# A fused pass over 32 blocks: two of six answers added by VectorE ahead of TensorE, releases made by ScalarE, two scales computed at once

## The chip, the cores and the metric

The kernel runs on one core of a Trainium2 chip. The metric is the device time of one execution in microseconds; the number for a kernel is the median over several executions. The profile and the trace come from one more execution, taken by the hardware profiler.

## The reference

Two layers, each a graph network followed by a mixture of experts, over 128 graphs of 64 nodes with 256 channels: 8192 tokens. Cut to what matters here:

```
# layer 0
x1  = x + gnn0(norm(x), adj)                 # 256 -> 1024 -> 256, rms norm, silu
xn1 = norm(x1)
top, idx = top_k(xn1 @ gate.T, 6);  s = softmax(top)       # 64 experts, 6 of them per token
mix = sum_k  s[k] * (xn1 @ lattice[idx[k]])                # six answers per token
h   = xn1 + mix @ out_w.T + out_b
x2  = x1 + norm(h) * ln_g + ln_b
# layer 1
hn  = norm(norm(x2)) * gamma + beta
x3  = x2 + norm(x2) + relu((adj @ hn) @ W_rel + b_rel + hn @ W_root)
xn3 = norm(x3)
top, idx = top_k(xn3 @ Wg + bg + bias, 2);  w = softmax(top)   # 8 experts, 2 per token
out = x3 + sum_k w[k] * (relu(xn3 @ W1[idx[k]] + b1) @ W2[idx[k]] + b2)
```

## The kernel before, in words

The tokens are handled in 32 blocks of 256 (two tiles of 128 rows). There are four passes.

1. A first pass over the blocks computes the graph network of layer 0, chooses six experts for each token, and sends a copy of the token, with its destination and its release (the softmax weight), to a table in DRAM that is sorted by expert. Sends are indirect DMAs whose descriptors GpSimd writes (`send`, L334).
2. An expert pass walks over the pages of that table, multiplies each page by the matrix of its expert, scales by the release and replies: an indirect DMA puts each answer into its place in `answer` (L341), six rows per token, already weighted.
3. The fused pass, to which the change belongs, walks over the blocks again. For each block it reads the six answers of each token (`load_y`, L974), adds and transposes them on TensorE (`mixture`, L994: six matmuls against the identity that accumulate in one PSUM region), multiplies by `out_w` (`out_proj`), finishes layer 0 (`layer_out_h`, `_a`, `_b`, `_c`), does the graph network of layer 1 (`flip_h`, `neighbours`, `convolve_a`, `convolve_b`), and chooses two experts and sends two copies per token (`residual1_a`, `residual1_b`, `flip3`, `gate1`, `choose1`, `count1`, `place1`, `send1`). The release of a copy here is the difference of the two top logits (`differ`, L296); the sigmoid is taken in the last pass. Each block has four sends, one per tile and rank, and each send has its own `differ`.
4. A last pass walks over the pages of the second table: two matmuls per page with relu between them, and an indirect DMA that adds the result to the output (L351).

The order in the fused pass is written out by hand for TensorE, VectorE and ScalarE: `staggered` (L486) runs over steps, and in each step over a list of stages, each a function with a lag in blocks. In step s a stage with lag l works on block s - l, so the stages of one step belong to different blocks and the list gives the order of each of the three engines' instructions. One step makes one stage of each kind. The list is at L1143: `load_y` has lag -3, `mixture` -2, `out_proj` -1, `layer_out_a` to `_c` 0, `neighbours` and `convolve` 1, `residual1` and `gate1` 2, `choose1` and `place1` 3, the later three `send1` 4. The queues of SyncE (all loads and stores of the pass) and GpSimd (the sends) are ordered by the framework's planner, which goes by program order and by when it reckons things ready.

Buffers: a tile pool gives each name a number of rotating buffers; a stage that writes a tile waits until the readers of the buffer's former content are done. `y` (six answers of a block, 12 KB per partition) has two buffers. The loads of `y` for block 5 and later wait until all replies of the expert pass have landed (`READY`, L512); those before read rows that are known to be complete.

In `layer_out_b` ScalarE takes two square roots of the variance of x2 (`spread` at L1031, L1035), one for the plain norm and one for the norm of the norm. In `layer_out_c` VectorE makes a scale and a shift from each (`scale_shift`, L62: a reciprocal at L67 and a product at L68) and adds one to the first scale (L1042). ScalarE then writes `hn` and `s` (L1045, L1049).

Of the kernel before, what the change touches and what calls it, by code (L numbers as in the profile page):

```python
# [9 lines left out]
F32 = mybir.dt.float32  # L10
# [5 lines left out]
AF = mybir.ActivationFunctionType  # L16
ALU = mybir.AluOpType
AX = mybir.AxisListType
PSUM = bass.MemoryType.PSUM
P = 128  # L20
# [58 lines left out]
class Router:  # L79
# [213 lines left out]

    def differ(self, t, k, top, xs):

        self.nc.vector.tensor_sub(xs[:, t, k, self.D + 1:self.D + 2], top[:, t, 1 - k:2 - k], top[:, t, k:k + 1])  # L296

    def normalize(self, w, den):
        nc = self.nc
# [186 lines left out]
def staggered(n, stages, first=0):  # L486

    for s in range(first + min(lag for lag, _ in stages), n + max(lag for lag, _ in stages)):
        for lag, f in stages:
            if first <= s - lag < n:  # L490
                f(s - lag)
# [3 lines left out]
def two_layer_gnn_moe_kernel(ctx: ExitStack, tc: tile.TileContext, a: dict, out: bass.AP):  # L495
    nc = tc.nc
    x_in, adjT = a["x"], a["adjT"]
    N, D = x_in.shape
# [4 lines left out]
    T = 2  # L503
# [5 lines left out]
    K0 = 6  # L509
    E1, F1, _ = a["L1_ffn_W2"].shape  # L510
    EARLY = 12
    READY = 5  # L512
    LOOK = 20
    KF = F1 // P
    ctx.enter_context(tc.manual_schedule(engines={ENG.PE, ENG.DVE, ENG.Activation}))
# [2 lines left out]
    small = ctx.enter_context(tc.tile_pool(name="small", bufs=3))  # L518
# [9 lines left out]
    ops = Ops(nc, small, ident, eps)  # L528
# [42 lines left out]
    def load_adjacency(b):  # L571
        at = adjacency[b % 4]
        for g in range(2):
            nc.sync.dma_start(out=at[g * G:(g + 1) * G, :, g * G:(g + 1) * G],
                              in_=adjT[2 * b * T + g:2 * (b + 1) * T:2].rearrange("t m n -> m t n"))
        return at
# [27 lines left out]
    with tc.tile_pool(name="c0", bufs=1) as c0, \  # L604
# [9 lines left out]
        blocks = [dict() for _ in range(NB)]  # L614
# [151 lines left out]
        def place(b):  # L766
# [3 lines left out]
            send(b, 0)  # L770
            if b == READY - 1:
                r0.look_back()
            if b == LOOK:
                r0.look(EARLY)

        def send(b, k):

            B = blocks[b]
            r0.release(k, *B["w"], B["xs"])
            r0.send(B["row"], B["xs"], b > LOOK, (k,))  # L780

# [46 lines left out]
        n = free[0] // 16  # L828
# [118 lines left out]
    with tc.tile_pool(name="c3", bufs=1, reuse_waits="tile") as c3, \  # L947
# [17 lines left out]
        blocks = [dict() for _ in range(NB)]  # L965
# [3 lines left out]

        def load_y(b):  # L970
            B = blocks[b]
            B["y"] = y = work.tile([P, T, K0, D], F32, name="y")
            for t in range(T):
                d = nc.sync.dma_start(out=y[:, t],  # L974
                                      in_=r0.answer[ts(b * T + t, P * K0), :].rearrange("(p k) d -> p k d", k=K0))
                if b < READY:
                    tc.declare_no_dep(d.ins, group="r0last", reason="in the first pages, or waited for above")

        def load3(b):
# [4 lines left out]
            nc.sync.dma_start(out=x1, in_=by_tile(x1_dram[b]))  # L984
            B["at"] = load_adjacency(b)

        def mixture(b):

            B = blocks[b]
            pt = psum.tile([P, KD, C], F32, name="ps")  # L990
            for t in range(T):
                for k in range(KD):
                    for i in range(K0):
                        nc.tensor.matmul(pt[:, k, ts(t, P)], lhsT=B["y"][:, t, i, ts(k, P)], rhs=ident,  # L994
                                         start=(i == 0), stop=(i == K0 - 1), is_transpose=True)
            B["accT"] = accT = work.tile([P, KD, C], F32, name="accT")
            nc.scalar.copy(accT, pt)

# [20 lines left out]
        def layer_out_b(b):  # L1019
            B = blocks[b]  # L1020
            h = B["h"]
            mv, rs = B["mvh"], B["rsh"]
            nc.vector.reciprocal(rs, rs)
            B["x2"] = x2 = work.tile([P, T, D], F32, name="x2")
            for t in range(T):
                nc.vector.scalar_tensor_tensor(h[:, t, :], h[:, t, :], mv[:, t, 0:1], ln_g,
                                               op0=ALU.subtract, op1=ALU.mult)
                nc.vector.scalar_tensor_tensor(x2[:, t, :], h[:, t, :], rs[:, t:t + 1], B["x1"][:, t, :],
                                               op0=ALU.mult, op1=ALU.add)
            B["mv2"] = mv = ops.stats(x2)  # L1030
            B["std2"] = ops.spread(mv)  # L1031


            B["rs2"] = rs2 = small.tile([P, T], F32, name="rs2")
            ops.std(rs2, mv[:, :, 1], 1e-10, 1.0 + 1e-5)  # L1035

        def layer_out_c(b):
            B = blocks[b]
            x2 = B["x2"]
            rs2, nm2 = ops.scale_shift(B["mv2"], B["rs2"])  # L1040
            rs, nm = ops.scale_shift(B["mv2"], B["std2"])
            nc.vector.tensor_add(rs, rs, one[:, :T])  # L1042
            B["hn"] = hn = work.tile([P, T, D], F32, name="hn")
            for t in range(T):
                nc.scalar.activation(hn[:, t, :], x2[:, t, :], AF.Identity, bias=nm2[:, t:t + 1], scale=rs2[:, t:t + 1])  # L1045

            B["s"] = s = work.tile([P, T, D], F32, name="s", bufs=3)
            for t in range(T):
                nc.scalar.activation(s[:, t, :], x2[:, t, :], AF.Identity, bias=nm[:, t:t + 1], scale=rs[:, t:t + 1])  # L1049
# [86 lines left out]
        def send1(b, i):  # L1136
# [4 lines left out]
            r1.send(B["row"], B["xs"], b > NB // 2, (k,), (t,))  # L1141

        staggered(NB, (  # L1143
            (-3, load_y),
            (-2, load3),
            (0, layer_out_h),
            (3, choose1),
            (-2, mixture),
            (1, flip_h),
            (3, count1),  # L1150
# [5 lines left out]
            (2, residual1_b),  # L1156
            (1, neighbours),
            (0, layer_out_b),
            (4, lambda b: send1(b, 3)),
            (1, convolve_a),  # L1160
            (2, flip3),
            (1, convolve_b),
            (2, gate1),
            (3, place1),
            (0, layer_out_c),
            (4, load_w2),
        ))
        r1.page_table(work.tile([P, 512], F32, name="scratch", bufs=1))
# [110 lines left out]
```

## Time and profile before

| | |
|---|---|
| median of 10 runs | 2055.2 us (2051.68 to 2060.04) |
| profiled execution | 2057.27 us, of which 2055.5 us are the span from the first to the last instruction |
| granted TensorE clock, mean | 0.972 |
| TensorE (PE) busy | 1926.8 us, 94% |
| TensorE weight loads (PEld) busy | 1678.8 us, 82% |
| VectorE (DVE) busy | 1199.6 us, 58% |
| ScalarE (ACT) busy | 1019.0 us, 50% |
| GpSimd (POOL) busy | 1164.2 us, 57% |
| fused pass, by the rows of L974 and L994 | from about 1132 us to about 1528 us of the span |
| busy in 1197.5 to 1474.0 us (276.5 us) | PE 276.36, DVE 250.92, ACT 178.79, POOL 106.04 us |

How to read it: the shares of the page are means over four passes with different limits, so they say little on one of them. The last row is the steady part of the fused pass alone. Busy time is the union of the instructions' spans; consecutive small instructions of one engine may overlap by some 0.08 us, and an instruction that needs the result of the one before it starts after that one's end. A busy PE is not TensorE at its peak, since its matmuls are pipelined. In rows of the timeline the columns are start and length in us, engine, line, operation, output and inputs with their shapes, the count, and in brackets the idle time of the engine just before and who ended it. In rows of the groups, the numbers after the bar are busy time in us and mean length in ns.

### The profile page before, as it was taken

What the parts mean: (1) busy time and instruction counts of PE and PEld (TensorE: products, weight loads), DVE (VectorE), ACT (ScalarE), POOL (GpSimd) and SP (SyncE); (2) the same over time, 40 slices, a digit from 0 to 9 for tenths busy, and PEclk for the clock granted to TensorE, in tenths of its full rate; (3) what the DMA queues carried; (4) which work ended last, traced back from release to release, by engine and by line L of the source; (5) the groups of instructions that cost most, each with busy time, mean ns of one, the idle gap of its engine ahead of it and who ended that gap; (6) DMA issues with size and microseconds to landing.
All of it is one profiled execution on the core that took longest, in us unless ns stands there. A gap on an engine that the chain in (4) does not pass through costs nothing. (4 is left out here: it accounts for less than half of the span.)

```text
span 2055.5 us, 37214 instructions
## 1 busy us (share of the span) xinstructions
PE 1926.8 (94%) x10516; PEld 1678.8 (82%) x10516; DVE 1199.6 (58%) x4205; ACT 1019.0 (50%) x2033; POOL 1164.2 (57%) x1134
## 2 busy tenths in 40 slices
PE   6999999999966989999999799999979999999996
PEld 5888888888864777888877688988868888888885
DVE  5899999999975333344333389999862222222221
ACT  4888888888841222222222266666643333333332
POOL 1377667767677777777777724333343444444443
PEclk9999999999977999999999899999989999999998
DMA  4244554544486988666665799788527666666664
GB/s 123 80 142 149 169 165 166 171 159 140 134 267 209 306 256 264 208 207 209 209 207 165 264 374 337 260 283 280 176 91 170 171 163 161 153 167 162 166 167 91
DMA packets 282561, 397.91 MB, mean 194 GB/s; under 512 B 56025, under 2 KB 236393, under 8 KB 282353
## 3 DMA queue, kind: packets, MB, share of 16 engines
q1 hardware_dynamic: 202880, 246.61, 39.4%
q0 software_dynamic: 64416, 136.14, 22.1%
q10 hardware_dynamic: 15056, 12.69, 1.9%
q8 instruction: 94, 1.54, 0.3%
q14 instruction: 115, 0.93, 0.2%
HBM read 222.84 MB, written 176.64 MB: 194 GB/s over the span
## 5 line engine op out<-in xcount | busy, mean ns | idle before, releaser
L334 POOL DMA_INDIRECT r0x<-xs,r0row x384 | 402.6, 1048 | 236.0 <-DVE lat L706 72.3
L341 POOL DMA_INDIRECT r0y<-px x404 | 393.4, 974 | 123.1 <-DMA r0y<-px 51.8
L918 PE MATMUL py<-lat,pxT 128*128 x1616 | 389.4, 384 | 16.6 <-ACT pxT L905 13.0
L351 POOL DMA_INDIRECT out_x<-py_s,px x138 | 215.1, 1559 | 294.5 <-DMA out_x<-py_s,px 203.0
L922 DVE TENSOR_SCALAR px<-py,px 128x256 f32<-128x256 f32 x404 | 176.9, 479 | 310.1 <-PE py L918 306.1
L918 PEld LDWEIGHTS py<-lat,pxT 128*128 128x128 f32 x1616 | 293.6, 192 | 57.4 <-ACT pxT L905 17.5
L905 ACT COPY pxT<-pt 128x512 f32<-128x512 f32 x202 | 118.1, 586 | 368.9 <-PE pt L903 252.0
L1217 ACT ACTIVATE phid<-ph,pw 128x256 f32<-128x256 f32 x276 | 130.9, 474 | 323.7 <-PE ph L1215 167.5
L1215 PE MATMUL ph<-pxT,pw 128*128 128x256 f32 x1104 | 251.5, 381 | 0.7 <-ACT pxT L1206 0.7
L1235 PE MATMUL py<-fw,phid 128*128 (+1 forms) x1104 | 249.8, 379 | 0.4 <-issue 0.4
L717 PE MATMUL ps<-lat 128*128 128x256 f32 x1024 | 238.5, 381 | 0.0
L1215 PEld LDWEIGHTS ph<-pxT,pw 128*128 128x128 f32 x1104 | 211.0, 191 | 30.1 <-ACT pxT L1206 1.1
L684 PE MATMUL ph<-lat 128*128 128x256 f32 x1024 | 232.4, 386 | 2.7 <-DVE lat L706 2.0
L1235 PEld LDWEIGHTS py<-fw,phid 128*128 128x128 f32 x1104 | 204.4, 190 | 25.6 <-issue 0.6
L334 POOL DMA_INDIRECT r1x<-xs,r1row x128 | 128.5, 1004 | 169.1 <-DVE xs L296 47.4
L684 PEld LDWEIGHTS ph<-lat 128*128 128x128 f32 x1024 | 195.2, 193 | 29.5 <-issue 2.4
L717 PEld LDWEIGHTS ps<-lat 128*128 128x128 f32 x1024 | 193.8, 192 | 24.9
L1229 DVE TENSOR_SCALAR p<-p 128x2 f32<-128x2 f32 x69 | 11.9, 172 | 224.4 <-ACT p L1228 224.4
L1238 DVE TENSOR_TENSOR py_s<-py,pb 128x512 f32<-128x512 f32 x69 | 47.8, 692 | 158.3 <-PE py L1235 149.7
L903 PE MATMUL pt<-ident,px 128*128 128x128 f32 x808 | 127.5, 277 | 12.4 <-DMA px<-r0x 12.0
L903 PEld LDWEIGHTS pt<-ident,px 128*128 128x128 f32 x808 | 101.1, 143 | 39.6 <-DMA px<-r0x 12.0
L994 PE MATMUL ps<-ident,y 128*128 128x128 f32 x768 | 96.3, 284 | 14.0 <-DMA y<-r0y 14.0
(303 smaller groups left out, 2981.9 us busy)
## 6 DMA issues: line engine op xcount, KB each, us to landing
px<-r0x SPq DMA_DIRECT2D x404, 129.0 KB
y<-r0y SPq DMA_DIRECT2D x64, 768.0 KB
pw<-in_L_ffn_W1b SPq DMA_DIRECT2D x69, 514.0 KB
px<-r1x SPq DMA_DIRECT2D x69, 258.0 KB
x<-x SPq DMA_DIRECT2D x64, 256.0 KB
pb<-in_L_ffn_b SPq DMA_DIRECT2D x69, 128.0 KB
r0x<-r0filler ACTq DMA_DIRECT2D x64, 129.0 KB
lat<-in_x SPq DMA_DIRECT2D x32, 256.0 KB
```

What stands on the lines that cost most here:

```text
L334: i = self.nc.gpsimd.indirect_dma_start(out=self.table[:, :], out_offset=bass.IndirectOffsetOnAxis(ap=row[:, t, k:k + 1], axis=0), in_=xs[ ...
L341: d = self.nc.gpsimd.indirect_dma_start(out=self.answer[:, :], out_offset=bass.IndirectOffsetOnAxis(ap=x[:, self.D:self.D + 1].bitcast(I32 ...
L351: i, d = f"{self.name}add{i}", self.nc.gpsimd.indirect_dma_start(out=self.total[:, :], out_offset=bass.IndirectOffsetOnAxis(ap=x[:, self.D ...
L684: nc.tensor.matmul(ph[:, c, :], lhsT=w1[:, k, ts(2 * j + c, P)], rhs=B["aggT"][:, k, :], start=(k == 0), stop=(k == KD - 1))
L717: nc.tensor.matmul(B["po"][:, t, :], lhsT=B["hT"][:, c, ts(t, P)], rhs=w2[:, c, :], start=False, stop=(t == T - 1 and c == KH - 1))
L903: nc.tensor.transpose(pt[:, k, ts(q, P)], Q["px"][:, q, ts(k, P)], ident)
L905: nc.scalar.copy(xT[:, :, :n * P], pt[:, :, :n * P])
L918: nc.tensor.matmul(py[:, q, :], lhsT=xT[:, k, ts(q, P)], rhs=lat[:, ds(regs["e"][(2 * j + q) % 4], 1), k, :].rearrange("p o d -> p (o d)") ...
L922: nc.vector.tensor_scalar(px[:, q, :D], py[:, q, :], px[:, q, D + 1:D + 2], None, op0=ALU.mult)
L1215: nc.tensor.matmul(ph, lhsT=w[:, k * F1 + c * P:k * F1 + (c + 1) * P], rhs=Q["xT"][:, k, :], start=(k == 0), stop=(k == KD - 1))
L1217: nc.scalar.activation(hid[:, c, :], ph, AF.Relu, bias=w[:, KD * F1 + c:KD * F1 + c + 1], scale=1.0)
L1235: nc.tensor.matmul(py[:, t, :], lhsT=Q["hid"][:, c, ts(t, P)], rhs=fw2[:, ds(e, 1), c, :].rearrange("p o d -> p (o d)"), start=(c == 0), s ...
```

## The change

- `load_y` moves from lag -3 to lag -4 and `y` gets a third buffer.
- A new stage `fold`, lag -3, last but one in the list (after `layer_out_c`). For blocks from 8 on, VectorE adds answers 4 and 5 of each token to answers 0 and 1, in place, in one instruction. `mixture` then accumulates four answers for these blocks instead of six.
- `differ` moves from VectorE (one subtraction) to ScalarE (one activation, -1 times the one logit plus the other as a bias).
- The two square roots of `layer_out_b` go into the halves of one tile; `layer_out_c` takes one reciprocal and one product over both halves instead of two each.

```diff
@@ differ
-        self.nc.vector.tensor_sub(xs[:, t, k, self.D + 1:self.D + 2], top[:, t, 1 - k:2 - k], top[:, t, k:k + 1])
+        self.nc.scalar.activation(xs[:, t, k, self.D + 1:self.D + 2], top[:, t, k:k + 1], AF.Identity,
+                                  bias=top[:, t, 1 - k:2 - k], scale=-1.0)
@@ constants
     READY = 5
+    FOLD = 2
@@ load_y
-            B["y"] = y = work.tile([P, T, K0, D], F32, name="y")
+            B["y"] = y = work.tile([P, T, K0, D], F32, name="y", bufs=3)
@@ before mixture
+        def fold(b):
+            B = blocks[b]
+            B["n"] = K0
+            if b > READY + 2:
+                B["n"] = n = K0 - FOLD
+                y = B["y"]
+                nc.vector.tensor_add(y[:, :, :FOLD], y[:, :, :FOLD], y[:, :, n:])
@@ mixture
-                    for i in range(K0):
+                    for i in range(B["n"]):
                         nc.tensor.matmul(pt[:, k, ts(t, P)], lhsT=B["y"][:, t, i, ts(k, P)], rhs=ident,
-                                         start=(i == 0), stop=(i == K0 - 1), is_transpose=True)
+                                         start=(i == 0), stop=(i == B["n"] - 1), is_transpose=True)
@@ layer_out_b
-            B["std2"] = ops.spread(mv)
-            B["rs2"] = rs2 = small.tile([P, T], F32, name="rs2")
-            ops.std(rs2, mv[:, :, 1], 1e-10, 1.0 + 1e-5)
+            B["std2"] = std = small.tile([P, 2, T], F32, name="std2")
+            ops.std(std[:, 0, :], mv[:, :, 1], 1e-5)
+            ops.std(std[:, 1, :], mv[:, :, 1], 1e-10, 1.0 + 1e-5)
@@ layer_out_c
-            rs2, nm2 = ops.scale_shift(B["mv2"], B["rs2"])
-            rs, nm = ops.scale_shift(B["mv2"], B["std2"])
+            both = small.tile([P, 2, T], F32, name="rs2")
+            nms = small.tile([P, 2, T], F32, name="nm2")
+            nc.vector.reciprocal(both, B["std2"])
+            nc.vector.scalar_tensor_tensor(nms, B["mv2"][:, :, 0].unsqueeze(1).to_broadcast([P, 2, T]), -1.0, both,
+                                           op0=ALU.mult, op1=ALU.mult)
+            rs, rs2 = both[:, 0, :], both[:, 1, :]
+            nm, nm2 = nms[:, 0, :], nms[:, 1, :]
             nc.vector.tensor_add(rs, rs, one[:, :T])
@@ the stages of the pass
-            (-3, load_y),
+            (-4, load_y),
...
             (0, layer_out_c),
+            (-3, fold),
             (4, load_w2),
```

## The prediction

> **What bounds the kernel now.** I first looked for the stretch that the change touches. The rows of L994, the reading of the answers, run from 1137.7 to 1476.1 us: the fused pass. The chain of waits there is TensorE alone, in steps of one period. One step of it:
>
> ```profile
> 1274.72 2.67 PE ps L994 x24
> 1277.39 0.44 PE ps L76 x4
> ...
> 1278.14 1.73 PE po L1005 x8
> 1279.87 1.73 PE pz L1066 x8
> ...
> 1284.84 0.92 PE pg L1112 x8
> 1285.77 0.27 PE ps L994 x2
> ```
>
> From one L994 to the next is 11.05 us with nothing of another engine between, so TensorE sets the step, and 24 matmuls in 2.67 us are 0.111 us each. That would make any cut of TensorE's work a gain. So next comes how near the other engines are, by stretches (columns: PE, PEld, DVE, ACT, POOL busy with counts, granted clock, DMA share, GB/s): a full step, and one at the end of the pass, when no answers are left to read.
>
> ```profile
> 1319.00:1330.00 11.00, 11.00 (x76) 9.85 (x75) 10.01 (x47) 7.10 (x16) 4.12 (x6) 1.00 0.81 262
> ...
> 1484.90:1495.70 10.80, 9.03 (x51) 7.31 (x50) 9.97 (x47) 6.28 (x15) 3.93 (x6) 1.00 0.21 73
> ```
>
> VectorE is busy 10.0 us of 11.0 in the full step, and what looks like 1 us of room is not room: many of its instructions start only when the one before has ended, some 0.03 us later. The timeline of VectorE shows the true room.
>
> ```profile
> 1328.10 0.39 DVE L327 CAST r1row<-r1rowf 128x4 int32<-128x4 f32 x1
> ...
> 1329.11 0.69 DVE L1011 TENSOR_TENSOR h<-po,xn 128x512 f32<-128x512 f32 x1
> 1329.99 0.17 DVE L1118 TENSOR_TENSOR logits<-pg,r_L_ffn_bg 128x16 f32<-128x16 f32 x1 [0.19 <-PE pg L1112]
> ...
> 1484.92 0.17 DVE L1118 TENSOR_TENSOR logits<-pg,r_L_ffn_bg 128x16 f32<-128x16 f32 x1 [0.22 <-PE pg L1112]
> ...
> 1494.58 0.16 DVE L67 RECIPROCAL bn_rs<-bn_sd 128x2 f32<-128x2 f32 x1
> 1494.77 0.16 DVE L68 SCALAR_TENSOR_TENSOR bn_nm<-bn_mv,bn_rs 128x2 f32<-128x2 f32 x1
> 1494.97 0.16 DVE L1042 TENSOR_TENSOR bn_rs<-bn_rs,one 128x2 f32<-128x2 f32 x1
> 1495.05 0.69 DVE L1011 TENSOR_TENSOR h<-po,xn 128x512 f32<-128x512 f32 x1
> 1495.66 0.16 DVE L1118 TENSOR_TENSOR logits<-pg,r_L_ffn_bg 128x16 f32<-128x16 f32 x1
> ```
>
> In a full step VectorE waits for another engine once, at the logits. From 1484.92 to 1495.66 it does the same 46 instructions while TensorE has no answers to read, and here the logits wait for nothing: 10.74 us is what VectorE needs for a step when nobody holds it. Its room in a full step is 11.05 - 10.74 = 0.31 us.
>
> **The change part by part.** *TensorE.* For blocks 8 to 31 the mixture reads four answers instead of six: 8 matmuls less, 8 x 0.111 = 0.89 us. TensorE's need falls to 11.05 - 0.89 = 10.16 us in 24 steps. That is all that is to be had, 21 us, and only if nothing else needs more than 10.16.
>
> *The fold, on VectorE.* One addition of 1024 elements per partition, both inputs in SBUF, float32. The same form is in the first pass (L694), and L1017 is its shorter relative:
>
> ```profile
> L694 DVE TENSOR_TENSOR lat<-lat 128x1024 f32<-128x1024 f32 x32 | 39.1, 1223 | 8.0 <-ACT lat L687 7.2
> ...
> L1017 DVE TENSOR_TENSOR x<-x,r_L_ffn_ln_b 128x512 f32<-128x512 f32 x25 | 16.5, 658 | 0.0
> ```
>
> It lasts 1.22 us. The next independent instruction starts 0.08 us before such a one ends (L1017 starts at 1323.24, lasts 0.66, its follower starts at 1323.82). So the fold takes 1.14 us of the queue; bounds 1.10 and 1.22. It is put behind the last scale of a step, so h, the logits, the choice and everything of the next step queue behind it, and TensorE's next mixture now waits for it. Its own wait, for an answer load issued a step earlier, is covered: in the steady steps nothing waited for y.
>
> *What leaves VectorE.* Four subtractions at L296: by the starts of the next instructions (0.04, 0.07, 0.05, 0.07 after them) 0.23 us, although each lasts some 0.15. And the scales: two reciprocals and two products become one each. From the first reciprocal (1494.19) to h (1495.05) is now 0.86 us; the new three instructions are the last three before h, 1494.58 to 1495.05, 0.47. Gain 0.39. Of this 0.12 is a stall: the cast at 1328.10 lasts 0.39 when a send's descriptors are written beside it (GpSimd from 1327.54 to 1328.51), 0.17 at 1195.15 when none are, and there the five instructions take 0.74. In the new order that send waits for ScalarE's release, made behind both square roots: by the row at 1493.46 that ends near 1493.95, and GpSimd starts sends about 0.28 later (1327.54 after 1327.26), 1494.2. The cast starts at about 1494.0 and ends before. I take the stall as gone; if it comes back, 0.12 more.
>
> VectorE's new need: 10.74 - 0.23 - 0.39 + 1.14 = 11.26 us (11.22 to 11.46). That is more than the 11.05 of now: in the 24 steps with a fold the step becomes VectorE's, and TensorE's 0.89 turns into a wait of 1.1 us per step at the mixture. 24 x 0.21 = +5.0 us (24 x 0.17 = +4.1 to 24 x 0.41 = +9.8).
>
> A rule against it is weighed here. L1017 lasts 658 ns in every step though a send's descriptors are being written during it (1322.52 to 1323.56), and L694 stayed at 1.22 with sends all around it, so I charge the fold nothing for GpSimd. The Trainium skill (SBUF — State Buffer, Who interferes with whom) says that a VectorE instruction with two SBUF inputs is blocked by a GpSimd instruction that reads SBUF. Were each fold held for one whole send of 0.97 us, the sum would be +28 us instead of +5.
>
> *ScalarE* gets four small activations: the 2-element ones last 0.29 and follow each other by 0.21, so 7.1 us become 7.9 to 8.3 of 11. One is on a path: the release of the fourth send stands between the square roots (1493.46) and the copy xn3T (1493.64), so gate and logits come 0.21 later. In the fold steps the logits have the fold ahead of them (1.14), which hides it. At the end it shows: steps 29 and 30 have no fold, VectorE needs 10.12, but gate ended at 1495.3 for logits possible at 1495.5, now 0.21 later and 0.11 earlier for the two subtractions ahead of it: about 10.7. Against 11.05 and 10.74 that is -0.4 in all (0 to -1.5).
>
> *SyncE.* A third buffer, loads of y one step earlier. In the filling of the pass TensorE waits for answers at 1159.35, 1163.59 and 1165.86 (0.40 + 0.78 + 0.73 = 1.9 us), which can shrink. But the load of block 5 is held until the last replies have landed (1181.28), and with the new order xn of block 3 (now issued at 1162.45) stands behind it; h of block 3 ran at 1184.50, with 1.06 us of idle after it. From -1.9 to +1.0; I take 0, since the load that gates it does not move. The DMAs are the same in number and bytes.
>
> **Sum.** +5.0 - 0.4 + 0 = +4.6. The profiled execution took 2057.27 us (span 2055.5 and 1.8 around it), 2.1 above the median of ten, 2055.2; the steps lost are the same in both, so the forecast is 2055.2 + 4.6 = 2059.8. Bounds: 4.1 - 1.5 - 1.9 = +0.7 and 9.8 + 1.0 = +10.8, so 2056 to 2066. About 0.2% (4.1 us) is what a measurement of this kernel can tell from no change, so this case alone lies on both sides of that line.
>
> **The rivals.** *Faster: the fold costs VectorE less than I charge.* VectorE's step is 10.12 plus the fold; at 0.93 us of fold nothing changes, and below that the kernel gains, down to TensorE's 10.16. At half my price (two elements a cycle, 0.61 us) the step is 10.73, 24 x -0.32 = -7.6: 2047; with a free fold 2034. For it: the operands lie in one tile, in long runs. Against it: L694 and L1017 both show one element per cycle. *The lock.* The cast, moved nearer to its send, is caught at the start of it: up to 0.97 us per step less the 0.17 of its own, 24 x 0.8 = +19, 2079. For it: 0.39 against 0.17 shows that it can be caught; against it: the 0.2 us between by the rows. *The clock.* TensorE, idle 1.1 us in 11.3, gets half its clock for a while. In the step after 1495.7 (TensorE idle 0.73 just before) the granted share is 0.84, and L1066 takes 3.06 us and L1077 2.36, 1.89 each in the steady steps. In the step before it a gap of 1.02 brought none:
>
> ```profile
> 1486.39 0.19 PE L217 MATMUL pos<-r1hot,r0tri 128*128 128x16 bf16 x2 [1.02 <-DVE r1hot L209]
> ```
>
> There TensorE was idle for over 1.7 us of 10.8, more than the fold steps leave; a slow stretch adds some 1.7 us to TensorE, of which 1.1 is covered, so 0.6 a step: +14, 2074. The Trainium skill (TensorE: Matmul & The Clock Gate, HAM oscillation) asks for gaps over about 3.4 us before the clock falls; the drop at the end of the pass came with gaps under 1.1 us.
>
> **How the numbers follow.** VectorE-bound as summed 0.77 (0.51 of it above +0.2%, 0.25 within, 0.01 below); faster by a cheaper fold 0.11; the lock 0.06; the clock 0.06. So slower 0.63, same 0.25, faster 0.12. The range takes the first case's bounds and reaches a little past them on both sides, 2054 to 2068, leaving out most of the three others.
>
> **What would show it.** Right: the period of L994 in the steady steps 11.2 to 11.4, TensorE with a wait of about 1 us for VectorE ahead of L994 in 24 steps, no wait of VectorE at the logits there, the fold at 1.22, the cast back at 0.17, granted clock 1.00. Wrong: a period under 11.0 (the fold or the removed work was mispriced), a cast of over 0.5, or a granted share below 1 in the steady steps.

## The result and the profile after

The median after is 2064.55 us (8 runs, 2062.09 to 2069.44) against 2055.62 us of the kernel before (28 runs with those taken beside it): +8.9 us, a ratio of 1.0047 with a 95% interval of 1.0038 to 1.0056. The change makes the kernel slower. The profiled execution took 2067.96 us, its span is 2066.1 us, and the mean granted clock is 0.974.

Line numbers after the diff are larger: the fold is L996, the mixture L1005, `out_proj` L1016, h L1022, the new scales L1053 and L1054, `xn3T` L1122, the gate L1128, the logits L1134, the cast L328, the release L296 (now on ScalarE).

The chain of waits in the fused pass, before a chain of TensorE alone, now reads so (start, length, what; one step):

```profile
1286.79 0.06 DVE y L996
1286.85 1.08 issue
1287.93 0.68 DVE h L1022
1288.62 0.09 DVE logits L1134
...
1295.06 0.48 DVE x L1039
```

Every piece of it is VectorE's. The 1.14 us of the first two lines are the fold: the "issue" is the rest of it, up to where h starts. Over the whole execution VectorE's share of the chain rises from 1% to 10% and TensorE's falls from 37% to 27%. The timeline of VectorE at the end of one step:

```profile
1297.43 0.17 DVE L328 CAST r1row<-r1rowf 128x4 int32<-128x4 f32 x1
1297.50 0.17 DVE L1053 RECIPROCAL rs<-std 128x4 f32<-128x4 f32 x1
1297.71 0.16 DVE L1054 SCALAR_TENSOR_TENSOR nm<-bn_mv,rs 128x4 f32<-128x4 f32 x1
...
1297.98 1.23 DVE L996 TENSOR_TENSOR y<-y 128x1024 f32<-128x1024 f32 x1
1299.13 0.68 DVE L1022 TENSOR_TENSOR h<-po,xn 128x512 f32<-128x512 f32 x1
1299.73 0.16 DVE L1134 TENSOR_TENSOR logits<-pg,r_L_ffn_bg 128x16 f32<-128x16 f32 x1
```

The fold lasts 1.23 us and occupies the queue for 1.15 (1297.98 to 1299.13). The logits, which ended the only wait of VectorE before, wait for nothing. The next logits come at 1310.93, 11.20 us later. TensorE has the gaps instead, two in each step:

```profile
1286.64 1.06 PE L1128 MATMUL pg<-m_L_ffn_Wg,xn3T 128*128 128x8 f32 x8 [0.34 <-ACT xn3T L1122]
1288.12 1.94 PE L1005 MATMUL ps<-ident,y 128*128 128x128 f32 x16 [0.42 <-PE pg L1128]
```

The second gap is put down to TensorE itself; the instruction that ended then is VectorE's fold (1286.79 plus 1.23 is 1288.02), whose end the mixture needs. By stretches (columns as above), a full step:

```profile
1309.90:1321.10 11.20, 10.45 (x68) 9.11 (x67) 10.48 (x42) 7.80 (x20) 4.49 (x5) 1.00 0.84 283
```

TensorE, busy 11.05 of 11.05 before, is busy 10.45 of 11.20, at full clock.

Where the time went, by the starts of the logits: in the 24 steps with a fold (third logits to 27th) 265.41 us before and 270.60 after, **+5.2**. From the first mixture to the third logits 70.75 and 71.87, **+1.1**. From the 27th logits to the last 51.16 and 52.02, **+0.9**. The fused pass begins 0.3 later, and the last pass begins 7.5 later in all. The rest, to 8.9, can't be placed: the last pass, whose code nobody touched, took 527.1 us in the profile before, 530.2 after, and between 526.2 and 534.7 in profiles of the experiments (all counted from its first product, `ph`).

### The profile page after: what moved, and what is told of

Same layout as the page of the kernel before. It is cut to its first block, busy times and chain, and to the rows that moved or that the text cites. A ratio compares the mean times of both kernels' runs of the same rounds, so it can differ in the third digit from the quotient of the medians.

```text
span 2066.1 us, 36720 instructions
## 1 busy us (share of the span) xinstructions
PE 1910.1 (92%) x10324; PEld 1658.6 (80%) x10324; DVE 1207.2 (58%) x4037; ACT 1039.9 (50%) x2161; POOL 1170.4 (57%) x1134
## 5 line engine op out<-in xcount | busy, mean ns | idle before, releaser
L335 POOL DMA_INDIRECT r1x<-xs,r1row x128 | 134.9, 1054 | 177.8 <-ACT xs L296 121.1
L689 ACT ACTIVATE lat<-ph,c_L_gnn_b 128x256 f32<-128x256 f32 x256 | 103.2, 470 | 12.2 <-PE ph L686 10.5
```

Source lines behind the costliest of these rows:

```text
L335: i = self.nc.gpsimd.indirect_dma_start(out=self.table[:, :], out_offset=bass.IndirectOffsetOnAxis(ap=row[:, t, k:k + 1], axis=0), in_=xs[ ...
```

## The experiments

Each time is compared with that of the kernel before beside it on the same chip. In the expectations of the first eight A is the theory of the prediction (VectorE's work per step sets the step), B that TensorE waits for an instruction put last, C that the loads at the start and ScalarE's releases count, D the clock. In one comparison (three answers folded, the scales apart, the releases back, the fold on GpSimd) every kernel took some 245 us more ahead of the fused pass, at half clock in many stretches there, and the kernel before took 2301.93 us beside them; what I compare of these four are the steps of the fused pass.

### The size of the fold

**No fold**, everything else of the change:

```
-            if b > READY + 2:
+            if b > NB:
```

> Theory A (VectorE's need of a step decides: 11.20 us with the fold, against 11.05 of TensorE before). Everything of the change but the fold; the mixture reads six answers. A: VectorE needs about 10.1 us, TensorE is the bound again at 11.05 us a step, and what is left is the start and the end of the pass, +1 to +3 us: 2057 to 2059. Rival C (the loss lies in the loads of the start and in ScalarE's releases, not in the fold): 2062 or more.

2058.07 us against 2057.33, 1.0006 (0.9995 to 1.0016); the step is back at 11.05, the 24 steps take 265.11. In the waits of that stretch VectorE waits for the gate again:

```profile
DVE logits L1134 <- PE pg L1128: 20.5, 23, 0.9
```

20.5 us in 23 waits are 0.89 a step. So without the fold VectorE needs at most 11.05 - 0.89 = 10.16 us. It is nearer 10.08, since logits that need not wait start 0.08 us before h ends (1299.73 above, where h ends at 1299.81). The lighter releases and scales are worth nothing by themselves: TensorE sets the step then.

**One answer folded instead of two:**

```
-    FOLD = 2
+    FOLD = 1
```

> The fold adds one answer to one (512 elements), the mixture reads five. A: VectorE needs 11.20 - 0.56 = 10.64 us, TensorE 11.05 - 0.44 = 10.61, so a step of about 10.65 us: 24 x -0.40 = -9.6 us against before, and the start and end on top: 2047 to 2050. Rival B (what costs is that TensorE waits for an instruction at the end of VectorE's step, whatever its length): 11.05 or more per step, 2057 or more. Rival C: the same loss as now less TensorE's gain, 2058 to 2060.

2050.33 us, 0.9963 (0.9950 to 0.9976): faster than both kernels. By groups (fused pass) and by stretches:

```profile
L996 DVE TENSOR_TENSOR y<-y 128x512 f32<-128x512 f32 x24 | 16.6, 693 | 0.0
```

```profile
1305.12:1315.79 10.67, 10.67 (x72) 9.48 (x71) 9.95 (x42) 7.68 (x20) 5.01 (x6) 1.00 1.00 346
```

The fold lasts 0.69 us, the step falls to 10.67 to 10.70, the 24 steps to 258.19 us (-7.2 against before), and neither engine waits in them: 1.4 us in all, TensorE 1.0 and VectorE 0.4. TensorE is busy in the whole step. The two engines meet here: four matmuls less for TensorE are 11.05 - 4 x 0.111 = 10.61.

**Three answers** (`FOLD = 3`):

> The fold adds three answers to three (1536 elements), the mixture reads three. Theory A (VectorE's work decides as long as the fold stands last): 11.20 + 512/0.96 ns = 11.73 us a step, 24 x 0.53 = +12.8 against the changed kernel, some 2077 (2074 to 2081), although TensorE needs only 9.7 us. Rival D (TensorE's idle 2 us a step halve its clock, and that costs on top): 2083 or more. Rival B (TensorE's saving counts): 2064 or less.

```profile
L996 DVE TENSOR_TENSOR y<-y 128x1536 f32<-128x1536 f32 x23 | 40.5, 1759 | 0.0
```

The fold lasts 1.76, the step 11.74, the ratio is 1.0079 (1.0047 to 1.0111). With one, two and three answers the step is 10.70, 11.20 and 11.74: each answer adds what the fold grows by (0.53 us a piece), and TensorE's lighter mixture takes nothing of it back. That is theory A in its plainest form. Of theory D the first half came true: the clock was at half for 3.41 us ten times in these 24 steps. It cost nothing on top, since the step, 11.74, stayed VectorE's.

### What was taken off VectorE

**The two scales apart, as before the change** (in `layer_out_b` and `layer_out_c`, the releases left on ScalarE):

```
+            rs2, nm2 = ops.scale_shift(B["mv2"], B["rs2"])
+            rs, nm = ops.scale_shift(B["mv2"], B["std2"])
```

> The changed kernel with the two scales made one after the other again. A: VectorE needs 0.27 us more (the stall of the cast is gone with the releases on ScalarE, so not 0.39), 11.47 us a step, +6.5: 2069 to 2073, the cast at 0.17 in the profile.

**The releases back on VectorE** (the scales left as one):

```
-        self.nc.scalar.activation(...)
+        self.nc.vector.tensor_sub(...)
```

> The changed kernel with the four releases back on VectorE. A: VectorE needs 0.23 us more, 11.43 us a step, 11.55 if the cast is caught by a send again as before the change: +5.5 to +8.4 against the changed kernel, 2070 to 2073. If the releases cost more on ScalarE, where they stand ahead of the copy that the gate waits for, than they free on VectorE: 2064 or less.

With the scales apart the step is 11.47 at full clock (11.55 to 11.76 in most steps in which the clock was at half for 3.4 us), 1.0057 (1.0031 to 1.0083). With the releases back it is 11.60, a little above what was expected, 1.0090 (1.0066 to 1.0113). Against the 11.20 of the change the scales are worth 0.27 us a step and the releases 0.40, against 0.39 and 0.23 in the prediction. The cast tells why; its row with the scales apart, and then its row with the releases back:

```profile
L328 DVE CAST r1row<-r1rowf 128x4 int32<-128x4 f32 x24 | 4.1, 170 | 0.8
```

```profile
L327 DVE CAST r1row<-r1rowf 128x4 int32<-128x4 f32 x24 | 8.9, 369 | 0.8
```

The stall of the cast leaves with the releases, not with the scales. One such place with the releases back (timeline):

```profile
1611.36 0.97 POOL L334 DMA_INDIRECT r1x<-xs,r1row  x1 [1.80 <-DVE r1run L313]
1611.92 0.38 DVE L327 CAST r1row<-r1rowf 128x4 int32<-128x4 f32 x1
1611.99 0.30 DVE L296 TENSOR_TENSOR xs<-r1top 128x1 f32<-128x1 f32 x1
1612.06 0.23 DVE L1052 RECIPROCAL rs<-std 128x4 f32<-128x4 f32 x1
1612.38 0.16 DVE L1053 SCALAR_TENSOR_TENSOR nm<-bn_mv,rs 128x4 f32<-128x4 f32 x1
```

Cast, release and reciprocal, begun one after the other, all end at 1612.29 or 1612.30, as GpSimd's writing of the descriptors does (1612.33). In the kernel after, the send near the cast starts at 1297.59, after the cast's start at 1297.43, since it waits for ScalarE's release; the cast takes 0.17. From the reciprocal to the product behind it are 0.32 us with the releases back and 0.21 in the kernel after, so the stall is worth 0.11. What in this place is held and why is open: the reduction just before (L325, 1611.69, beside the same send) took its usual 0.19.

### The place of the fold

**The fold in mid-step**, listed after `residual1_b` instead of after `layer_out_c`:

> The changed kernel with the fold in the middle of the step, after residual1_b, instead of last. A: VectorE does the same work in another order, so steps of 11.20 us again and 2064.5 (2062.5 to 2066.5). B: TensorE's mixture no longer waits for VectorE's last instruction, steps fall below 11.0, 2058 or less.

2075.72 us, 1.0092 (1.0079 to 1.0106): some 10 us slower than with the fold last, at the same work (the 24 steps take 281.5 us). No theory had that. The timeline at the end of such a step:

```profile
1277.90 0.48 ACT L36 ACTIVATE std<-bn_mv,eps 128x2 f32<-128x2 f32 x2 [2.00 <-DVE r1run L314]
1278.29 0.28 ACT L296 ACTIVATE xs<-r1top 128x1 f32<-128x1 f32 x1
1278.47 0.56 ACT L1122 COPY xn3T<-ps 128x512 f32<-128x512 f32 x1
...
1279.09 1.06 PE L1128 MATMUL pg<-m_L_ffn_Wg,xn3T 128*128 128x8 f32 x8 [1.25 <-ACT xn3T L1122]
1280.01 2.84 PE L1005 MATMUL ps<-ident,y 128*128 128x128 f32 x16
1280.19 0.17 DVE L1134 TENSOR_TENSOR logits<-pg,r_L_ffn_bg 128x16 f32<-128x16 f32 x1 [0.27 <-PE pg L1128]
```

Read from the top: ScalarE has waited 2.00 us for VectorE (r1run L314, just behind its last statistics), takes two square roots, a release, and only then the copy; TensorE has waited 1.25 us for the copy; the logits wait for the gate. From the square roots to the logits are 2.3 us, and VectorE has too little left to do in them. With the fold last, its 1.15 us lie just there.

**The same with the copy first**: `flip3` listed ahead of `layer_out_b`, so that on ScalarE the copy no longer stands behind the square roots and the release.

> The kernel with the fold in the middle of the step (after residual1_b), and the flip3 step listed ahead of layer_out_b, so that on ScalarE the copy of xn3T stands ahead of the two square roots of the second norm and of a release instead of behind them. The path theory says that in the mid-step kernel the loop closed over VectorE's last statistics, two square roots (0.48 us), a release (0.28), the copy (0.56), the gate (1.06) and the logits; with the copy ahead, the copy no longer waits for the statistics, TensorE's 1.25 us wait ahead of the gate goes, and the step falls to VectorE's work, 11.2 us: 24 steps of 269 to 271 us, and a time 8 to 10 us above the kernel before, as the change itself. The rival, that the fold in mid-step costs by what it delays on VectorE behind it (h, residual and statistics later, so that TensorE waits for hT and z), says that the copy's place does nothing and the step stays at 11.6 to 11.9: 17 to 20 us above the kernel before.

2069.05 us against 2057.25, 1.0053 (1.0040 to 1.0066); the step is 11.24 to 11.25, the 24 steps take 271.40, and the 1.25 us wait ahead of the gate is gone (timeline, then by stretches):

```profile
1286.85 0.95 PE L1128 MATMUL pg<-m_L_ffn_Wg,xn3T 128*128 128x8 f32 x8
```

```profile
1288.02:1299.26 11.24, 10.48 (x69) 9.14 (x67) 10.52 (x42) 7.97 (x20) 4.76 (x5) 1.00 0.92 328
```

The path is shown: with the same fold in the same place, taking the copy out from behind ScalarE's square roots brings the step from 11.57 and more back to VectorE's work. The edit also moves the transposes of `flip3` forward on TensorE; the wait that went is the one for ScalarE's copy. The whole is no better than the change, because the last steps pay: the stretch from the 27th logits to the last took 55.0 us instead of 52.0. VectorE waited there at three logits (4.23, 4.84 and 4.15 us), in the kernel after at two for as long (5.65 and 4.21).

### The loads at the start

**The two loads in the other order**, `load3` listed ahead of `load_y`, with two answers folded and with one:

> The changed kernel with the load of xn and x1 listed ahead of the load of y, so that block 3's xn no longer stands behind the load that waits for the last replies. A: the steps stay at 11.20; VectorE's wait of 6.9 us for xn at the start goes, the pass starts 1 to 3 us earlier: 2061.5 to 2063.5. C: most of the loss goes, 2058 or less.

> The change with one answer folded instead of two, and load3 listed ahead of load_y as in the run on the order of loads. By VectorE's work the steps are those of one answer folded, 10.67 to 10.70 us and 258 us for 24; the order of loads gave nothing that lasted with two answers, and if that holds here the ratio is that of one answer folded, 0.9963 within 0.001. If the start counts where TensorE is the bound, 1 to 2 us less: 0.9954 to 0.9958.

With two answers 2066.37 us, 1.0038 (1.0024 to 1.0052): a miss of what A and C expected, and not told apart from the change (1.0047, 1.0038 to 1.0056). With one answer 2050.51, 0.9965 (0.9949 to 0.9982): the same as without the new order. The first logits did come earlier (with one answer at 1184.66 instead of 1187.26 us), but the first interval after them grew from 10.22 to 11.81; 0.49 us of it is the mixture's wait for answers now read later. From the first mixture to the third logits 0.8 and 1.5 us were gained, and neither shows in the medians.

### The fold on GpSimd

```
-                nc.vector.tensor_add(y[:, :, :FOLD], y[:, :, :FOLD], y[:, :, n:])
+                nc.gpsimd.tensor_add(y[:, :, :FOLD], y[:, :, :FOLD], y[:, :, n:])
```

> The changed kernel with the fold on GpSimd instead of VectorE. By VectorE's and TensorE's work alone the step falls to 10.2 us; the path from x2's statistics over ScalarE, gate and logits, which showed in the run with the fold in mid-step, allows 10.5 to 10.6: 2048 to 2051. Against it: GpSimd also makes the sends, and VectorE's instructions with two SBUF inputs may be held while GpSimd reads SBUF; if each fold holds VectorE for its own length, 2070 or more.

The slowest of all: 1.0114 (1.0086 to 1.0143), steps of 10.65 to 13.71 us, six in a row of 12.99 among them. VectorE loses more than the fold that it no longer does. Its groups there (160, 659 and 169 ns in the kernel after, in this order), and one place of the timeline:

```profile
L1058 DVE TENSOR_TENSOR rs<-rs,one 128x2 f32<-128x2 f32 x23 | 24.2, 1051 | 0.8
L1028 DVE TENSOR_TENSOR x<-x,r_L_ffn_ln_b 128x512 f32<-128x512 f32 x23 | 23.6, 1027 | 0.0
...
L207 DVE CAST r1which<-r1idx 128x4 f32<-128x4 uint32 x23 | 11.9, 517 | 0.8
```

```profile
1681.72 3.09 DVE L1058 TENSOR_TENSOR rs<-rs,one 128x2 f32<-128x2 f32 x1
1682.40 2.38 POOL L996 TENSOR_TENSOR y<-y 128x1024 f32<-128x1024 f32 x1
```

The small addition ends at 1684.81, GpSimd's fold at 1684.78. The three groups are longer by 0.89, 0.37 and 0.35 us, 1.6 a step in the mean, more than the 1.15 saved. Over the 24 steps (288.8 us, 270.6 with the fold on VectorE) that is some 11 of the 18 us; VectorE's waits at the logits, 5.2 us, are part of the rest. In the six steps of 12.99 it is L1058 alone: 11.20 - 1.15 + (3.09 - 0.16) = 12.98, and 12.99 is measured. That the addition's span begins before GpSimd's fold (at 1681.72, beside a send) stays unexplained.

## Why the prediction was right, point by point

**The engine that sets the step: right.** With the fold the step is VectorE's. The chain says so, and one, two and three answers put it beyond doubt, since the step follows VectorE's fold and not TensorE's matmuls.

**The step's length: right, 11.20 where 11.26 was forecast;** +5.2 us in 24 steps where +5.0 was. A few steps are longer than 11.20 (12.12 the longest), so the total is above 24 x 0.15 = 3.6: that the totals agree so well is in part luck. The fold's price, 1.14 from the row of L694, measured 1.15. The rival of a cheaper fold is ruled out by that.

**The removed work: the sum right, its split wrong.** 0.23 + 0.39 was forecast; the runs show 0.40 for the releases and 0.27 for the scales. The stall of the cast was booked to the scales, while the reason given for its going (the send waits for ScalarE's release) belongs to the releases. Its size was right, 0.12 forecast and 0.11 measured; by the starts of the next instructions the four subtractions are 0.22, and the rest of the 0.40 is spread over other rows. The parts now add up: 11.20 - 1.15 + 0.40 + 0.27 = 10.72, where 10.74 was read for VectorE's need before.

**The lock: right that a send does not hold the fold.** The fold from 1297.98 to 1299.21 had GpSimd write descriptors beside it, in the kernel after from 1297.59 to 1298.55 and again from 1298.86, and the 24 folds have a mean of 1226 ns, where L694 has 1223. The Trainium skill (SBUF — State Buffer, Who interferes with whom) says that a VectorE instruction with two SBUF inputs contends with a GpSimd instruction that reads SBUF, and not with one that only writes it. With sends, no fold here shows contention; with an addition on GpSimd it is plain (L1058, 0.16 to 1.05 us in the mean). So the +28 us that the prediction worked out for a fold held by a send did not come, while with the fold on GpSimd VectorE was held.

**TensorE's wait: right in kind, smaller.** 0.34 and 0.42 us in two places, 0.76 instead of 1.1 in one; TensorE was busy 10.45 us, not 10.16.

**What hides ScalarE's new release: right, and more than the prediction saw.** It named the fold as the cover of the later gate. The mid-step run gives the price of losing that cover, 10 us. The prediction knew only the 0.21 us of the release on this path; the loop closed over it makes the step 0.37 longer (11.57), and more where the clock falls (24 x 0.37 = 8.9 of the 10.9 us by which these 24 steps are longer).

**The start: mis-sized.** 0 was taken, between -1.9 and +1.0. Measured +1.1. The event was named (xn of block 3 behind the load that waits for the replies), and this was the wait, with a second one for the answers themselves:

```profile
1188.03 0.69 DVE L1022 TENSOR_TENSOR h<-po,xn 128x512 f32<-128x512 f32 x1 [6.94 <-DMA xn<-xn]
```

```profile
1185.38 4.48 PE L1005 MATMUL ps<-ident,y 128*128 128x128 f32 x24 [2.35 <-DMA y<-r0y]
```

The xn was issued at 1181.79 and landed near 1187.9, some 6 us for a transfer among the loads of y. The 1.06 us of idle after h that the prediction set against it did not cover that. The runs with the loads in the same order differ in this stretch, though: 71.1 us with no fold, 71.6 in mid-step, 71.9 with one answer and 72.8 with the copy first, against 70.75 before, so the term is not known to better than 1 us.

**The tail: wrong, but within what varies.** -0.4 was forecast, +0.9 measured; the two steps that it named took 10.41 and 11.29 us, the second with TensorE at half clock from 1492.8 (eight matmuls of L1016 took 3.50 us instead of 1.89), together 0.1 less than before. The loss came behind them, most of it in the last interval but one (10.67 instead of 9.81), with the clock at half for 6.83 us from 1513.3. The same stretch took 51.4 us with no fold, 50.8 with one answer and 49.9 with the two loads exchanged, so this term is not known to better than 1 us.

**The clock: right for this change.** It stayed at 1.00 in nearly all steps with a fold, with gaps of 0.34 and 0.42; it fell once, to half for 3.41 us from 1380.2, behind a gap of 1.33. That the rival was no idle one is shown below.

So of the 4.3 us by which the forecast (+4.6) fell short of +8.9, the steps are 0.2, the start 1.1, the tail 1.3, and the rest, 1.7, can't be placed.

## What to carry to other kernels

Before work is moved from the engine that bounds to its neighbour, read the neighbour's need in a step in which nobody holds it; its busy share hid that it had 0.31 us of room and not 1. Move only as much as makes the two needs equal: here one answer of six, 10.67 us for both, was a gain of 0.37%, and two a loss of 0.47%. In a loop over several engines the place of added work counts as much as its amount: last, it lies over the others' path; in the middle it lengthens it.

## What the hardware showed that was not expected

TensorE's clock fell behind gaps of 1.25 us. With the fold in mid-step the granted clock fell to one half for 3.41 us after some of these gaps, again and again (1233.1, 1257.0, 1280.9, 1315.0 us and on), and with the copy first, where the gaps were gone, not once between 1160 and 1500 us: in mid-step the mixture that starts at 1280.01 took 2.84 us instead of 1.94, and that step 11.80 us instead of 11.57. Gaps of 0.76 in two pieces, in the kernel after, did not do it. The Trainium skill (TensorE: Matmul & The Clock Gate, HAM oscillation) speaks of gaps over about 3.4 us; these were shorter. But the length of a gap alone does not decide. With three answers folded the clock fell ten times with gaps of 0.68 and 0.95 on either side of the gate, and with the fold on GpSimd (both in the comparison with the slower start) it stayed at 1.00 through seven gaps of 1.84 us, one every 12.99, of which this is the fourth:

```profile
1686.79 0.19 PE L217 MATMUL pos<-r1hot,r0tri 128*128 128x16 bf16 x2 [1.84 <-DVE r1hot L209]
```

What else it takes is open.

GpSimd needs 2.38 us for the addition that takes VectorE 1.23, and holds some of VectorE's instructions beside it until it ends, a cast with one input (L207, 0.17 to 0.52 us in the mean) among them. An L1028 that had begun first (1541.83, GpSimd's addition at 1541.98) kept its 0.66 us, and there the addition took 2.71.
